# A four-layer decoder on one core: the order of instructions planned by a second simulator

## The chip, the core and the metric

The kernel runs as one program on one core of a Trainium2 chip. The time is the device time of one execution in microseconds. Before the change it was measured in 12 runs; one further execution was recorded with the hardware profiler, and all durations in this document come from such recorded executions.

## The reference

The input is `x`, 8 sequences of 256 tokens of 256 numbers, and a context `ctx_768` of 8 x 120 rows of 192 numbers. Four layers follow one another; each has a self-attention or its like, a cross-attention to the context, and a feed-forward part. After each of the twelve parts stands a residual sum and a layer norm:

```python
x = _layernorm(x + _L0_attn_ref(x, ...))
x = _layernorm(x + _L0_xattn_ref(x, ctx_768, ...))
x = _layernorm(x + _L0_ffn_ref(x, ...))      # 8 experts, the best one per token
...                                          # L1: rope attention, cross-attention, 32 experts and a shared one
...                                          # L2: attention with compressed keys, quantized cross-attention
x = _layernorm(x + _L2_ffn_ref(x, ...))
x = _layernorm(x + _L3_attn_ref(x, ...))
x = _layernorm(x + _L3_xattn_ref(x, ctx_768, ...))
x = _layernorm(x + _L3_ffn_ref(x, ...))      # fixed-point MLP with a piecewise linear gelu
```

The part that takes longest is layer 2's feed-forward. It looks up 4 heads x 8 experts of 4096 for each token by product keys, and adds a gated MLP:

```python
sx, ix = jax.lax.top_k(sim[0], TOPK)         # sim: queries against 128 keys, per half and head
sy, iy = jax.lax.top_k(sim[1], TOPK)
scores, pk = jax.lax.top_k(all_scores, TOPK) # all_scores: 8 x 8 sums of sx and sy
w = jnp.einsum('btd,bthkd->bthk', hidden_states, down_embed[indices])
w = jax.nn.silu(w) * jax.nn.softmax(scores, axis=-1)
experts_states = jnp.einsum('bthk,bthkd->btd', w, up_embed[indices])
mlp = jax.nn.silu(hidden_states @ Wg.T) * (hidden_states @ Wu.T) @ Wd.T
```

Layer 3's attention is a gated 3-tap convolution with a linear scan along the sequence and a layer norm of its own; its cross-attention has 8 heads of 64 on 120 context rows.

## The kernel before

**Tiles.** The 2048 tokens lie in 16 tiles of 128 tokens (`X`), with their transpose `xT` beside them. A batch is one sequence, two tiles. Matrix products go through `mm` (L144), transposes of X through `transpose_into_xT` (L185, copied by L186), and every part ends with `finish`: the sum of the residual, batch-norm statistics (L175, L176), a reciprocal root, X (L199) and its transposes. The reciprocal root is two POOL instructions (L153, L155) in the attention parts and a Newton iteration on DVE (L158 to L166) elsewhere.

**Who decides the order.** The program names operations in source order and writes no order of its own for the engines. A planner of the framework simulates the five engines and their queues: each engine takes, of the operations whose inputs are there by the simulated clocks, the one that stands first in the source. What comes out is a fixed list of instructions for PE, DVE, ACT, POOL and SP (the queue that issues most transfers), with waits on semaphores between them. On the chip each engine works off its own list in that order.

**The attention parts** (l0_attn, l1_attn, l1_xattn, l2_attn) run over pairs of heads' scores, sums and output products; before the scores' exponentials, each row's lower bound is transposed into the queries by `lower16` (L544), and after them sums are divided on DVE (`divided16`, L588 to L600) and projected (`project_o`, whose sum is L630).

**The border to l1_ffn.** In l1_xattn, `choose` (L764 to L768) takes the experts of each batch as soon as its X is there. At the same time ACT sums the absolute values of the quantized weights of l2_xattn (L800, L802). l1_ffn then adds these over partitions with one POOL instruction, `partition_all_reduce` (L1252); the steps that scale by it stand in `ternary` (L1983). `route1` (L1137 to L1235) makes the lists of tokens for 32 experts, and the experts follow: a gather of tokens (L988), two transposes (L1006), two products, and a store of y. Behind the loop, `prepare_l2_xattn` (L2015 to L2042) quantizes and multiplies the context for the next part, with transposes at L2040; `routed_batches` gathers the stored rows (L988, `w<-yd`) and adds them to X.

**l2_ffn** is one loop over the 8 batches with background work in generators:

```python
experts = self.expert_batches(w, spare[:, : 8 * D], pool, work, ps, general)
for b in range(B):
    experts(b, later)
    later = chain(convolve(b), attend(b))
```

In `batch(b, later)` stand the MLP's products, then for each of the two tiles groups of four gathered rows (L988): dot products with X (L1599), activation and weight (L1655, L1656), a diagonal matrix (L1660), and a product on PE that adds the row times its weight (L1661). Between these steps `next(later)` pulls the next piece of the background: first the routing of batch b + 1 (`route`: query products, `sim` by L1388, the best 8 by L1391 and L1392, and so on to L1468), then layer 3's convolution of batch b - 1 (`convolve`, called C below) and its cross-attention (`attend`, A below: score products L1781, their maximum L1789, exponentials L1792, transposes L1797, sums L1803). C0 and A0 are those of batch 0, and so on. The convolution and the attention share their buffers from batch to batch, one of each, so that C0, A0, C1, A1 ... C7, A7 are a serial chain. The fixed-point part (`fixed_point`, L1829) follows with units of half a batch.

The planner is given to the program in `kernel`, at the line that the diff changes:

## Time and profile before

| | us |
|---|---|
| median of 12 runs | 2550.86 |
| lowest and highest run | 2528.13, 2563.61 |
| profiled execution, whole | 2545.84 |
| its span | 2544.1 |
| PE busy | 2064.2 (81%) |
| DVE busy | 1549.6 (61%) |
| ACT busy | 933.6 (37%) |
| POOL busy | 681.4 (27%) |
| granted PE clock, mean | 0.88 |

A busy share is that of the time in which an instruction of the engine was running, over the span. A high share of the whole span can hide stages in which the engine waits, so the stages are looked at one by one. They were, by start and end in us: l0_attn 22 to 210, l0_xattn to 264, l0_ffn to 528, l1_attn to 750, l1_xattn to 922, l1_ffn to 1139, l2_attn to 1397, l2_xattn to 1547, the loop of l2_ffn to 2285, the rest of layer 3's attention parts to 2450 and the fixed-point part to 2545. The granted clock is the share of full speed that the TensorE was given in a stretch; matmul durations are longer where it is low.

### The profile page before, as it was taken

What the parts mean: (1) busy time and instruction counts of PE and PEld (TensorE: products, weight loads), DVE (VectorE), ACT (ScalarE), POOL (GpSimd) and SP (SyncE); (2) the same over time, 40 slices, a digit from 0 to 9 for tenths busy, and PEclk for the clock granted to TensorE, in tenths of its full rate; (3) what the DMA queues carried; (4) which work ended last, traced back from release to release, by engine and by line L of the source; (5) the groups of instructions that cost most, each with busy time, mean ns of one, the idle gap of its engine ahead of it and who ended that gap; (6) DMA issues with size and microseconds to landing.
All of it is one profiled execution on the core that took longest, in us unless ns stands there. A gap on an engine that the chain in (4) does not pass through costs nothing. (4 is left out here: it accounts for less than half of the span.)

```text
span 2544.1 us, 38544 instructions
## 1 busy us (share of the span) xinstructions
PE 2064.2 (81%) x14051; PEld 1505.8 (59%) x14051; DVE 1549.6 (61%) x5022; ACT 933.6 (37%) x2056; POOL 681.4 (27%) x731
## 2 busy tenths in 40 slices
PE   8998689699989978957787685778788888886885
PEld 5665588545557656824455433656666676665674
DVE  4666200276667756545666787774866875853775
ACT  2332233233334352212333242334443444442652
POOL 1022221221111205443321014333423423420232
PEclk9999699899999978968899786888888888896898
DMA  2001442200011116811100003112211211220000
GB/s 88 2 1 58 171 153 76 73 9 1 1 68 33 49 56 190 246 59 34 34 18 30 33 17 96 49 56 62 67 49 50 76 48 57 83 82 8 1 17 18
DMA packets 69045, 147.54 MB, mean 58 GB/s; under 512 B 15864, under 2 KB 39560, under 8 KB 66928
## 3 DMA queue, kind: packets, MB, share of 16 engines
q0 software_dynamic: 30528, 81.81, 10.9%
q1 hardware_dynamic: 35564, 59.47, 7.1%
q10 hardware_dynamic: 2756, 3.72, 0.4%
q8 instruction: 113, 1.85, 0.3%
q14 instruction: 84, 0.69, 0.1%
HBM read 175.56 MB, written 23.76 MB: 78 GB/s over the span
## 5 line engine op out<-in xcount | busy, mean ns | idle before, releaser
L988 POOL DMA_INDIRECT rows<-in_l2f_table_dram,index x240 | 248.1, 1034 | 301.5 <-PE po L1661 115.3
L144 PE MATMUL pp<-xT,w 128*128 128x256 f32 (+1 forms) x672 | 197.4, 439 | 4.6 <-DVE hT L1135 1.7
L144 PE MATMUL ph<-xeT,we 128*128 128x128 f32 (+1 forms) x992 | 175.8, 319 | 19.2 <-DMA we<-in_l0f_experts_dram,wrow 14.6
L185 PE MATMUL pt<-ident,X 128*128 128x128 f32 x352 | 78.7, 343 | 130.8 <-DVE X L199 113.0
L1661 PE MATMUL po<-rows,diag 128*128 128x256 f32 x480 | 142.7, 435 | 45.3 <-issue 29.8
L144 PEld LDWEIGHTS ph<-xeT,we 128*128 128x128 f32 x992 | 151.1, 200 | 40.7 <-DMA we<-in_l0f_experts_dram,wrow 15.9
L144 PEld LDWEIGHTS pp<-xT,w 128*128 128x128 f32 x672 | 140.6, 218 | 34.8 <-issue 7.2
L600 POOL TENSOR_TENSOR aT<-sides,inv 128x256 f32<-128x256 f32 x64 | 46.6, 729 | 421.3 <-DVE sides L598 327.8
L185 PEld LDWEIGHTS pt<-ident,X 128*128 128x128 f32 x352 | 49.7, 167 | 169.5 <-DVE X L199 80.8
L186 ACT COPY xT<-pt 128x512 f32<-128x512 f32 x88 | 51.4, 586 | 261.8 <-PE pt L185 257.5
L1661 PEld LDWEIGHTS po<-rows,diag 128*128 128x128 f32 x480 | 97.2, 214 | 76.3 <-issue 43.1
L988 POOL DMA_INDIRECT xe<-xd,take x87 | 86.2, 991 | 182.7 <-DVE y L1112 77.0
L144 PE MATMUL py<-we,hT 128*128 128x256 f32 x496 | 129.7, 386 | 1.2 <-DVE hT L1135 1.2
L1112 DVE TENSOR_TENSOR y<-py,we 128x256 f32<-128x256 f32 x23 | 9.8, 425 | 196.2 <-PE py L144 196.2
L564 ACT ACTIVATE e<-sc 128x512 f32<-128x512 f32 (+1 forms) x146 | 77.4, 602 | 99.7 <-PE sc L492 66.8
L1106 ACT ACTIVATE hT<-ph,we 128x128 f32<-128x128 f32 x184 | 65.7, 367 | 117.8 <-PE ph L144 86.1
L492 PE MATMUL sc<-kv,qv 32*128 32x128 f32 (+2 forms) x1520 | 103.6, 316 | 3.3 <-ACT e L564 1.9
L1660 ACT ACTIVATE diag<-ident,dots 128x128 f32<-128x128 f32 x224 | 75.4, 393 | 79.0 <-PE po L1661 22.2
L144 PE MATMUL sc<-xT,w 128*128 128x512 f32 x216 | 103.0, 626 | 1.3 <-ACT xT L186 1.3
L199 DVE TENSOR_SCALAR X<-z,ln_mv,rs_y 128x256 f32<-128x256 f32 x176 | 67.0, 423 | 58.5 <-POOL rs_y L155 58.1
L1599 DVE SCALAR_TENSOR_TENSOR junk<-rows,X 128x256 f32<-128x256 f32 x224 | 93.8, 419 | 12.7 <-DMA rows<-in_l2f_table_dram,index 7.0
L492 PEld LDWEIGHTS sc<-kv,qv 32*128 32x128 f32 x1520 | 80.2, 189 | 33.5 <-issue 26.2
(570 smaller groups left out, 5180.3 us busy)
## 6 DMA issues: line engine op xcount, KB each, us to landing
we<-in_l1f_experts_dram SPq DMA_DIRECT2D x32, 384.0 KB
yd<-y SPq DMA_DIRECT2D x32, 256.0 KB
w<-in_l2x_w_dram SPq DMA_DIRECT2D x1, 4096.0 KB
v<-v SPq DMA_DIRECT2D x16, 243.8 KB
rows<-in_l2f_table_dram,index POOLq DMA_INDIRECT x240
yd<-y SPq DMA_DIRECT2D x23, 128.0 KB
X<-in_x_dram SPq DMA_DIRECT2D x8, 256.0 KB
xd<-X ACTq DMA_DIRECT2D x8, 256.0 KB
```

Source lines behind the costliest of these rows:

```text
L144: self.nc.tensor.matmul(out, lhsT=lhsT, rhs=rhs, start=n == 0, stop=n == last and bias is None)
L185: nc.tensor.transpose(pt[:, c, j, :], self.X[:, i0 + j * step, c * P : (c + 1) * P], self.ident)
L186: nc.scalar.copy(self.xT4[:, :, i0 : i0 + step + 1 : step, :], pt)
L199: nc.vector.tensor_scalar(self.X[:, i, :], z[:, j, :], mv[:, j, 0:1], r[:, j : j + 1], ALU.subtract, ALU.mult)
L492: nc.tensor.matmul(sc[: shape[0], part], lhsT=lhsT, rhs=rhs, start=mask is None, stop=True, skip_group_check=True)
L564: lambda r, sc: nc.scalar.activation(e0[m][:n0, r], sc, AF.Exp),
L600: nc.gpsimd.tensor_tensor(out, split(both), split(inv), ALU.mult)
L988: self.nc.gpsimd.indirect_dma_start(out=out, out_offset=None, in_=table, in_offset=bass.IndirectOffsetOnAxis(ap=index, axis=0), **({} if r ...
L1106: nc.scalar.activation(hT[:, g + f, :], ph[:, f, :], AF.Gelu, bias=b1[:, g + f : g + f + 1])
L1599: nc.vector.scalar_tensor_tensor(junk, row, 1.0, x, ALU.mult, ALU.mult, accum_out=out)
L1660: nc.scalar.activation(diag, sel, AF.Copy, scale=dots[:, k : k + 1])
L1661: nc.tensor.matmul(po, lhsT=diag, rhs=rows[:, k, D:], start=False, stop=(g, k) == (groups[-1][0], size - 1))
```

## The change

The planner is told to use the framework's other simulator, the timeline simulator, when it decides which instruction comes next. No operation is added, removed or altered; the lists of instructions have the same operations in other orders, and with them other waits.

```diff
-    with tile.TileContext(nc) as tc:
+    with tile.TileContext(nc, schedule_with_timeline_sim=True) as tc:
         build(tc, ins, out)
```

How far instructions move in their engine's list, the two lists laid side by side: on PE, 1531 of the 1700 of the l2_ffn stage (by 59 places on average), 421 of 620 in l1_ffn (by 29), 216 of 257 in the fixed-point part (by 13), 253 of 439 in l2_xattn (by 4), and 227 to 417 of about 1100 in each attention part (by 1 to 2.5). On DVE, 1868 of 2094 in the l2_ffn stage (by 69). SP's list moves 13 of 212. POOL's moves little, but for the two tiles of a batch: before, the gathers of the second tile stand around POOL's steps of the next routing, after, behind them. The table loads of ACT go from 72 to 70.

## The prediction

> **What bounds the kernel now.** The page's busy table gives PE 81% of the span, DVE 61%, ACT 37%, POOL 27%. As the change moves order and nothing else, I needed to know stage by stage whether an engine is full (then order is worth little) or whether engines wait for each other (then order is worth what they wait). So the second view is the windows view, cut at the stage borders. The columns are the stretch in us, its length, busy us of PE, PEld, DVE, ACT and POOL, the granted PE clock, the DMA share and GB/s:
>
> ```profile
> 922.00:1139.00 217.00, 166.87 (x902) 128.56 (x903) 128.13 (x324) 60.17 (x138) 91.36 (x91) 0.82 0.53 157
> 1139.00:1397.00 258.00, 206.04 (x2064) 123.42 (x2062) 157.07 (x355) 88.91 (x152) 72.07 (x90) 0.89 0.09 26
> 1547.00:2285.00 738.00, 590.89 (x2728) 467.22 (x2726) 511.91 (x2410) 299.08 (x741) 272.02 (x261) 0.85 0.23 64
> 2285.00:2450.00 165.00, 127.61 (x555) 101.12 (x556) 97.94 (x241) 81.53 (x141) 22.86 (x12) 0.81 0.02 4
> ```
>
> These are l1_ffn, l2_attn, the l2_ffn loop, and what remains of layer 3's cross-attention behind it. The loop is 738 of 2544 us and no engine fills it: PE has 147 us free, DVE 226. Inside it the background chain C0, A0, C1, A1 ... C7, A7 (a convolution batch, then a context batch) is serial, and expert work is laid beside it. I cut the loop where each background batch starts on DVE. Two loaded phases (C4, A4) and two in which the chain runs almost alone (C6, A6):
>
> ```profile
> 2084.50:2135.60 51.10, 41.49 (x153) 31.40 (x152) 37.23 (x171) 18.63 (x54) 28.40 (x27) 0.80 0.29 82
> 2135.60:2180.80 45.20, 41.14 (x226) 32.53 (x225) 30.78 (x153) 21.15 (x47) 5.30 (x5) 0.92 0.13 38
> 2279.00:2302.00 23.00, 10.96 (x46) 7.87 (x44) 16.01 (x54) 4.51 (x11) 0.17 (x3) 0.86 0.00 0
> 2302.00:2345.00 43.00, 32.29 (x129) 24.37 (x129) 12.98 (x50) 11.59 (x29) 0.00 (x0) 0.62 0.05 12
> ```
>
> A context batch lasts 45 us loaded and 43 us alone: expert work beside it is nearly free. A convolution batch lasts 51 loaded and 23 alone. What is waited for in the loop is seen in the view of groups, by form (busy us, mean ns, idle us before and its releasers):
>
> ```profile
> L1661 PE MATMUL po<-rows,diag 128*128 128x256 f32 x480 | 142.7, 435 | 45.3 <-issue 29.8 <-ACT diag L1660 13.9 <-DMA rows<-in_l2f_table_dram,index 1.4
> L1391 DVE MAX8 top<-sim 128x8 f32<-128x128 f32 x128 | 32.0, 280 | 22.1 <-ACT sim L1388 21.8
> L1789 DVE TENSOR_REDUCE nm<-s 128x4 f32<-128x480 f32 x24 | 14.9, 650 | 18.7 <-PE s L1781 18.4
> ```
>
> **The l2_ffn loop.** In the changed order each batch's routing and its expert products stand one phase earlier against the chain; at the last expert product PE has passed C5 and A4 where before it had passed C6 and A5. On DVE the maximum of context scores (L1789) stands behind the batch's whole routing chain (L1391 to L1468). I counted the instructions of each phase in both orders and multiplied them by their mean durations in this trace. The larger of PE and DVE per phase, before/after, in us: up to C0 95/109.6; C0 65.5/46.1; A0 44.3/67.4; C1 51.4/44.2; A1 40.8/65.1; C2 44.5/46.5; A2 38.7/51.6; C3 44.5/41.9; A3 38.7/49.9; C4 44.5/36.7; A4 38.7/21.6; C5 45.5/26.3; A5 40.2/21.6. Before, these sum to 632.3 and the phases lasted 732.8: a factor of 1.16. After, the last three hold less than their latency. They cannot go below the rows of the chain alone: 43.5 for A4 and A5, 28 for C5 (23 alone plus its remaining expert work), 115 together. The ten loaded phases sum to 559.0.
> With 1.16 throughout that is 648 + 115 = 763, +30. By kind it is less: convolution phases lasted 1.07 times their larger sum before, context phases from A2 on 1.17, and the first phase was partly latency (127.5 for 95), so that I let half of its 14.6 more work show: 135 + 1.07 x 215.4 (C0 to C4) + 1.17 x 234.0 (A0 to A3) + 115 = 754, +21. I take **+20**. Ends: factor 1.05 (C0) gives 587 + 115 = 702, -31; 1.22 (A0 and A1 had 1.24 and 1.25) gives 797, +64. The loss has one cause: expert work is pulled forward out of A4, C5 and A5, where it was nearly free, into A0 and A1, which then have PE and DVE both at 65 and more.
> [...]
>
> **The end.** Behind the loop are C7, A7 and the fixed point's batches of some 20 us. After, the fixed point stands further ahead of A7 (parts of 5, 6 and 7 are left, before 3 to 7). The 165 us stretch has PE free for 37; a small part of that is got back: **-5** (-10 to 0).
>
> **The border to l1_ffn.** Before, POOL has batch 7's reciprocal root (L153, L155) ahead of the all-reduce (L1252), after behind it; and on DVE seven scalar steps (L1983) that wait for the all-reduce stand ahead of batch 7's last sum (L630), statistics and X. From the timeline view, DVE and then POOL (start, us, engine, line):
>
> ```profile
> 914.66 0.69 DVE L630 TENSOR_TENSOR z<-sc,biased 128x512 f32<-128x512 f32 x1 [3.82 <-PE sc L144]
> 917.48 0.73 DVE L199 TENSOR_SCALAR X<-z,ln_mv,rs_y 128x256 f32<-128x256 f32 x2 [1.13 <-POOL rs_y L155]
> ```
> ```profile
> 914.50 0.19 POOL L802 TENSOR_TENSOR w<-w,more 128x1 f32<-128x1 f32 x1 [2.86 <-ACT size L800]
> 916.44 0.22 POOL L153 TENSOR_SCALAR rs_v<-ln_mv 128x2 f32<-128x2 f32 x1 [1.75 <-DVE ln_mv L176]
> 923.15 0.49 POOL L1252 PARTITION_ALL_REDUCE w_scale<-w  x1 [5.71 <-issue]
> ```
>
> The all-reduce can start 5.71 us after L802 ends at 914.69 and is over at 920.9; seven steps of about 0.1 us bring L630 to 921.7 instead of 914.66: 7.0 later. Queued behind it are X, its transposes, the gate logits, L767 and the whole of route1; the experts' first gathers wait for that. After also loads POOL's other code once more between L1252 and L153; no row prices that, from 0 to another 5.71, which would put L153 at 926.6, 10.2 later. **+8**.
> [...]
>
> **The end of l1_ffn.** The changed order takes the preparation of the next cross-attention into the expert loop: 8 bit-linear products at 0.55 to 0.6 us, 16 transposes at L2040 of 0.43 and two small steps, 123.6 to 133.6 us of PE in a stretch (970 to 1086) where it is 111 of 116 busy. Before they lay from 1086 to 1107, under the last store and its gathers. Two groups of PE from 986 to 1130:
>
> ```profile
> L2040 PE MATMUL pp<-ident,w 128*120 128x128 f32 x16 | 3.9, 427 | 0.0
> L185 PE MATMUL pt<-ident,X 128*128 128x128 f32 x4 | 1.2, 448 | 14.4 <-DVE X L199 14.4
> ```
>
> That cover is given up and nothing takes its place: PE only waits longer at L185. **+9** (+4 if it first fills the 5 free us, +12 if DVE's conversions hold PE as well).
>
> **Attention stages.** 90 to 93% PE, and an instruction moves one to two places on average. The last transposes of lower16 (L544) go about 8 matmuls later. PE waits 12.0, 3.5 and 2.2 us there in l2_attn, l1_attn and l0_attn; half of 17.7 is **-8** (-15 to +5, as the late reciprocals could hold up the transposes). l0_ffn, l0_xattn and l2_xattn (DVE 124.6 of 150) keep their order but for a few places: 0 (-3 to +3). SP's queue moves 13 instructions; ACT's table loads go from 72 to 70 on the way, 3 us of ACT at most.
>
> **Sum.** 20 - 5 + 8 + 9 - 8 = +24 on the profiled 2545.84, 2570. The median of the runs is 5 above that execution, so against it the same step reads 2575.
>
> **Rivals.** *Faster:* the factor of the loop is no constant but the price of in-order waits that the other order avoids. For it: 29.8 of L1661's 45.3 us are "issue", PE waiting for nothing that shows, and L1391 and L1789 wait 40 us for engines which are not full. Against it: DVE's L1789 gets more work ahead of it, not less. Price: 1.05 gives -31 + 4 of the rest = -27, 2519. It decides from 1.084 down (-12 in the loop). *No change:* the chain sets both orders and the work moved forward is what idles anyhow; factor 1.085 to 1.11, 2546 (0.3% or 7.6 us is what a measurement can tell). *Slower by far:* routing ahead of L1789 stalls the chain each time, 1.22: +64 + 4 = 2614. That the change does nothing is excluded, as the queues differ: 1531 of 1700 PE instructions of the loop are moved.
>
> **Chances.** Forecast (2554 to 2595) 0.46, far slower 0.14, no change 0.11, faster 0.29. Range 2510 to 2630: the ends of the loop with the smaller terms on the same side in part. The sign hangs on the loop's factor: 1.084 is the point, the phases of before show 1.05 to 1.25 and 1.16 as their mean, so most of the chance lies above. The forecast's own range has the loop at +4 to +45.
>
> **What would show it.** Right: A4, C5 and A5 at PE under 0.7 busy with 43, 28 and 43 us and the last expert product before A5; A0 and A1 at 70 to 80 us; L630 of batch 7 some 7 us later against the stage's start; PE idle at L185 after l1_ffn above 14.4. Wrong: A0 and A1 under 68, L1661's idle below 20, the loop (first routing to C6) at 705 or less. If the attention stages move by over 15 us, the terms of places were mis-sized.

## The result, and the profile after

The changed kernel takes 2699.58 us (median of 11 runs, 2693.51 to 2705.60), the kernel before 2547.9 (46 runs): a ratio of 1.0597 [1.0578, 1.0616], 6% slower. The forecast was 2570, its range 2510 to 2630: the direction was right, the size was missed by 130 us. The profiled execution took 2701.38 us.

```profile
PE 2222.5 (82%) x14051; PEld 1622.7 (60%) x14051; DVE 1561.5 (58%) x5022; ACT 935.8 (35%) x2054; POOL 682.8 (25%) x731
```

The first thing to see is this line of the page. No operation was added, and DVE, ACT and POOL are busy within 12 us of before, but PE is busy 158 us more (2222.5 for 2064.2). PE does not wait more (477.0 us of its span idle, before 479.9); it is at work for longer with the same 14051 instructions.

Where? The windows view of the changed kernel, cut at l1_attn, l1_ffn with l2_attn, and the loop of l2_ffn (the columns are those of the prediction), and below it l1_attn of before, whose line was not shown:

```profile
542.00:813.00 271.00, 262.56 (x2048) 159.72 (x2046) 142.61 (x296) 87.15 (x158) 41.53 (x56) 0.88 0.02 9
1172.00:1516.00 344.00, 283.82 (x2123) 162.78 (x2121) 171.84 (x401) 92.46 (x158) 96.04 (x116) 0.82 0.11 31
1656.00:2434.00 778.00, 615.85 (x2723) 500.08 (x2722) 520.97 (x2408) 300.11 (x739) 272.28 (x261) 0.81 0.21 61
```
```profile
528.00:750.00 222.00, 205.85 (x2039) 125.80 (x2037) 142.94 (x295) 85.13 (x153) 41.49 (x52) 0.99 0.02 6
```

In l1_attn PE has the same 2040 instructions, 57 us more of busy time, and 0.88 of the clock where it had 0.99. All stages of the two recorded executions, in us, cut at the last ACT instruction of each (so that l1_ffn ends at 1107 before, and what follows up to 1139 counts with l2_attn):

| stage | before | after | difference | forecast |
|---|---|---|---|---|
| start | 22 | 16 | -6 | 0 |
| l0_attn | 190 | 202 | +12 | in -8 |
| l0_xattn | 51 | 43 | -8 | 0 |
| l0_ffn | 266 | 282 | +16 | 0 |
| l1_attn | 223 | 272 | +49 | in -8 |
| l1_xattn, with part of the border | 170 | 181 | +11 | in -8, +8 |
| l1_ffn and l2_attn | 476 | 520 | +44 | +9, in -8 |
| l2_xattn | 150 | 144 | -6 | 0 |
| l2_ffn and the end | 996 | 1040 | +44 | +20 - 5 |

**Attention: the rotation of the row groups.** `four_banks` writes two kinds of products. Masks (L487) are 128*128 in the profile's lines, all rows of the PE array; score products (L492) are 32*128, one of four row groups, and the source issues four masks and then score products that take the four row groups in turn. The profile has two instructions for each score product (1024 in l1_attn for the program's 512). From the timeline view (start, us, engine, line, tile and the number of instructions that follow one another), before and then after:

```profile
537.49 0.61 PE L487 MATMUL sc<-causal,ident_bf 128*128 128x256 bf16 x4
538.03 1.15 PE L492 MATMUL sc<-kv,qv 32*128 32x256 f32 x16
```
```profile
554.92 0.28 PE L487 MATMUL sc<-causal,ident_bf 128*128 128x256 bf16 x1
555.13 1.13 PE L492 MATMUL sc<-kv,qv 32*128 32x256 f32 x4
...
577.23 0.39 PE L487 MATMUL sc<-later_k,ident_bf 128*128 128x256 bf16 x1
577.55 2.07 PE L492 MATMUL sc<-qv,kv 32*128 32x256 f32 x4
```

Before, 16 instructions of 32x256, which the program gives to the four row groups in turn, take 1.15 us. After, the timeline planner puts a mask, the four instructions of one row group, the next mask, and so on: these 4 alone take 1.13 us, so that the 16 before ran side by side. And 22 us later four of one row group take 2.07. The windows view of after shows the clock around that place, 0.91 up to 562 us and 0.50 behind it:

```profile
553.00:562.00 9.00, 8.03 (x53) 5.39 (x53) 6.97 (x12) 0.10 (x1) 0.00 (x0) 0.91 0.00 0
562.00:592.00 30.00, 30.00 (x136) 18.13 (x134) 6.96 (x11) 4.48 (x9) 0.00 (x0) 0.50 0.00 1
592.00:772.00 180.00, 178.05 (x1650) 107.52 (x1648) 114.06 (x234) 66.04 (x120) 29.44 (x36) 0.99 0.01 1
```

From 562 to 592 PE is busy in all of the 30 us, and its clock is 0.50. In l1_attn and l1_xattn together, counted in steps of 3 us, PE runs 87 us below 0.75 while it is over 90% busy; before it was 18. Without such windows the loss is seen where busy time is compared at equal counts, in the groups of PE in l1_attn, before and then after:

```profile
L492 PE MATMUL sc<-qv,kv 32*128 32x128 f32 (+1 forms) x408 | 27.9, 342 | 0.1
```
```profile
L492 PE MATMUL sc<-qv,kv 32*128 32x128 f32 (+1 forms) x408 | 50.6, 396 | 0.0
```

The mean of one instruction rises only from 342 to 396 ns, as instructions that overlap are each counted whole (408 of 342 ns are 139.5 us, in 27.9 us of busy time); the group's busy time rises from 27.9 to 50.6 us. In the two programs' lists I counted rounds, a round being successive 32-row products none of which uses a row group a second time, and switches between products of the whole array and those of a part. l1_attn has 512 such products, so 128 rounds at least: before 131 rounds and 128 switches, after 197 and 208. Over the four attention parts after has 199 more rounds and 202 more switches.

**The loop.** Two groups of the loop that the prediction showed, after (L1661 had waited 45.3 us, 29.8 of them for "issue", and L1789 18.7):

```profile
L1661 PE MATMUL po<-rows,diag 128*128 128x256 f32 x480 | 132.5, 411 | 21.5 <-issue 11.1 <-ACT diag L1660 10.3
L1789 DVE TENSOR_REDUCE nm<-s 128x4 f32<-128x480 f32 x24 | 15.2, 648 | 13.4 <-PE s L1781 13.1
```

Both wait less, and still the loop from the first routing to C6 lasts 777.2 us, before 732.8. By phase, from C0: 41.5, 81.6, 46.3, 75.2, 43.5, 63.0, 43.0, 62.0, 45.4, A4 50.4, C5 37.5, A5 42.7. PE is also busy for longer at equal counts, 616 us for 591, at a clock of 0.81 for 0.85; whether these 25 us or the waits come first was not separated. The chain is served late. A3 of after begins at 2194.1; from its timeline, PE, ACT and DVE:

```profile
2202.09 3.62 PE L144 MATMUL s<-xT,w 128*128 128x256 f32 x16
2207.99 0.70 PE L1781 MATMUL s<-kT,qT 64*128 64x120 f32 x4 [2.29 <-ACT qT L1774]
...
2204.72 1.28 ACT L1134 ACT_TABLE_LOAD   x1
2207.35 1.08 ACT L1774 ACTIVATE qT<-s 128x512 f32<-128x512 f32 x2
...
2213.51 0.64 DVE L1789 TENSOR_REDUCE nm<-s 128x4 f32<-128x480 f32 x1
```

Its first products stand behind ten instructions of MLP products on PE, its query copy (L1774) behind two table loads and a silu on ACT, and its maximum behind the routing chain on DVE, which works through L1435 to L1496 from 2204.7 to 2213.6. The first maximum starts 19.4 us after the start of the phase, in before's A3 9.45.

**The border.** POOL and then DVE of after:

```profile
982.73 0.49 POOL L1252 PARTITION_ALL_REDUCE w_scale<-w  x1 [5.65 <-issue]
990.09 0.24 POOL L153 TENSOR_SCALAR rs_v<-ln_mv 128x2 f32<-128x2 f32 x1 [6.88 <-issue]
```
```profile
983.69 0.68 DVE L630 TENSOR_TENSOR z<-sc,biased 128x512 f32<-128x512 f32 x1
991.20 0.74 DVE L199 TENSOR_SCALAR X<-z,ln_mv,rs_y 128x256 f32<-128x256 f32 x2 [5.83 <-POOL rs_y L155]
```

L630 stands 8.2 us behind L802's start where it stood 0.2 behind it; then POOL waits 6.88 us for nothing that shows ahead of L153. route1 begins 20.8 us after the end of L802, before 8.1.

### The profile page after: what moved, and what is told of

Its sections match the earlier page's. It is cut to its first block, busy times and chain, and to the rows that moved or that the text cites. A ratio compares the mean times of both kernels' runs of the same rounds, so it can differ in the third digit from the quotient of the medians.

```text
span 2699.5 us, 38557 instructions
## 1 busy us (share of the span) xinstructions
PE 2222.5 (82%) x14051; PEld 1622.7 (60%) x14051; DVE 1561.5 (58%) x5022; ACT 935.8 (35%) x2054; POOL 682.8 (25%) x731
## 5 line engine op out<-in xcount | busy, mean ns | idle before, releaser
L144 PE MATMUL pp<-xT,w 128*128 128x256 f32 (+1 forms) x672 | 184.7, 423 | 8.3 <-DVE hT L1135 6.9
L185 PE MATMUL pt<-ident,X 128*128 128x128 f32 x352 | 76.8, 346 | 116.7 <-DVE X L199 109.1
L600 POOL TENSOR_TENSOR aT<-sides,inv 128x256 f32<-128x256 f32 x64 | 46.6, 729 | 463.8 <-DVE sides L598 411.9
L1661 PE MATMUL po<-rows,diag 128*128 128x256 f32 x480 | 132.5, 411 | 21.5 <-issue 11.1
L492 PE MATMUL sc<-kv,qv 32*128 32x128 f32 (+2 forms) x1520 | 144.2, 338 | 0.7 <-DVE sides L598 0.7
L185 PEld LDWEIGHTS pt<-ident,X 128*128 128x128 f32 x352 | 50.3, 170 | 148.3 <-issue 82.8
L492 PE MATMUL sc<-qv,kv 32*128 32x128 f32 (+2 forms) x1352 | 138.1, 366 | 0.0
L492 PEld LDWEIGHTS sc<-kv,qv 32*128 32x128 f32 x1520 | 108.4, 205 | 31.2 <-issue 24.4
L1661 PEld LDWEIGHTS po<-rows,diag 128*128 128x128 f32 x480 | 95.1, 205 | 42.6 <-issue 14.8
L492 PEld LDWEIGHTS sc<-qv,kv 32*128 32x128 f32 (+1 forms) x1352 | 91.8, 202 | 30.4 <-issue 22.1
```

Of the source, the lines that this page charges most:

```text
L144: self.nc.tensor.matmul(out, lhsT=lhsT, rhs=rhs, start=n == 0, stop=n == last and bias is None)
L185: nc.tensor.transpose(pt[:, c, j, :], self.X[:, i0 + j * step, c * P : (c + 1) * P], self.ident)
L492: nc.tensor.matmul(sc[: shape[0], part], lhsT=lhsT, rhs=rhs, start=mask is None, stop=True, skip_group_check=True)
L600: nc.gpsimd.tensor_tensor(out, split(both), split(inv), ALU.mult)
L1661: nc.tensor.matmul(po, lhsT=diag, rhs=rows[:, k, D:], start=False, stop=(g, k) == (groups[-1][0], size - 1))
```

## The experiments

The five sets ran on four chips, and the time of before itself is not the same in all of them: 2554.63, 2453.41, 2451.57, 2544.48 and 2544.54 us. In a kernel that was recorded in two sets (`mix` below) most of the difference lies in the l2_ffn loop. Each kernel is therefore compared with before of its own set, and stage times only within a set or with the set named. The theories in the expectations go by letters: A is the lost rotation, D the prediction's own cause (expert work pulled forward into the wrong phases), G that the clock falls to half where one row group is alone at work, J that no single queue carries the loop's loss, K that rotation, border and loop are all of it; other letters are their rivals.

### Is it the rotation?

`pin_banks` is the changed kernel, with the products of one call of `four_banks` held in source order by dependencies of order alone:

```diff
+        run = self.in_order()          # each product after the one before, on the same queue
         if mask is not None:
             for sc in banks:
-                nc.tensor.matmul(
+                run(nc.tensor.matmul(
...
         for parts in zip(*(heads(r) for r in range(4))):
             for sc, (part, lhsT, rhs) in zip(banks, parts):
-                nc.tensor.matmul(
+                run(nc.tensor.matmul(
```

> The changed kernel (timeline planner), with the matmuls of each four_banks call chained on PE in source order (masks, then the row groups 0, 32, 64, 96 in turn), issue order only. Theory A (the new order broke the rotation over the four 32-row groups of the PE array, so that matmuls which ran side by side run one after another): l1_attn back from 271 to about 225 us, l2_attn from 297 to about 260, l0_attn and l1_xattn some 10 shorter each, granted clock in l1_attn back from 0.88 to above 0.95, in all about 110 less: 2590. Rival B (the loss of the attention parts is in what waits on DVE and ACT, not in PE's order): within 15 us of the changed kernel, 2700.

Measured: 2615.02 us, 1.0227 [1.0195, 1.0259] of before; 2590 was expected. Rounds and switches are back at 129 and 136 in l1_attn, the stage at 227 us with a clock of 0.98, l0_attn at 193. The comparison with after was made later within one set:

> The changed kernel unaltered, beside its variants on one chip: 1.06 of the kernel before on a chip where that takes 2550; where it takes 2450, the kernels that keep this loop order have lost 105 us in the loop instead of 44, so 1.08 to 1.09 (2640 to 2680).

> pin_banks beside the changed kernel on one chip: 80 to 95 us below it, all of it in l0_attn, l1_attn, l1_xattn and l2_attn.

Measured: 2697.07 (1.0582 [1.0517, 1.0647]) and 2608.38 (1.0255 [1.0222, 1.0287]). The rotation is worth 89 of the 153 us that after loses there: l0_attn 207 to 193, l1_attn 266 to 229, l2_attn 346 to 313, while the loop stays (775.5 and 779.1).

### What the rotation's loss is made of

Four kernels with the order of the planner before, in which only `four_banks` differs. `bank_by_bank` issues all score products of one row group before those of the next; `half_masks` splits each mask in two and issues both halves first, as the control for `masks_between`, which puts the second halves in the middle of the products; `mask_and_bank` issues a mask, then all products of its row group, and so on, which is the pattern seen at 555 us. In `half_masks` the first half of each mask does not enter the sums.

```diff
 # bank_by_bank
-        for parts in zip(*(heads(r) for r in range(4))):
-            for sc, (part, lhsT, rhs) in zip(banks, parts):
+        for sc, parts in zip(banks, (heads(r) for r in range(4))):
+            for part, lhsT, rhs in parts:
 # half_masks                             # masks_between
+        masks(0)                          +  for at, parts in enumerate(...):
+        masks(1)                          +      if at % n == 0: masks(at // n)
 # mask_and_bank: bank_by_bank, with each mask directly ahead of its row group's products
```

> The kernel before (default planner), four_banks written bank by bank: all matmuls of row group 0, then of 32, 64, 96, chained on PE; the switches between full-array and 32-row matmuls stay as they were. Theory A: each attention part 40 to 100 us longer (the changed kernel lost 50 in l1_attn with a quarter of the broken rounds), in all +150 to +350: 2700 to 2900, with the granted clock of these parts down to 0.9 or less. Rival C (the switches between full-array and 32-row matmuls cost the time, not the rotation): within 15 us of before, 2550.

> Control for the next: the kernel before, each mask matmul of four_banks cut into two halves, all of them ahead of the 32-row matmuls, chained on PE; no more switches than before. All theories: 8 short mask matmuls instead of 4 longer ones per call, +10 to +30 us in all.

> As half_masks, but the second half of the masks stands in the middle of the 32-row matmuls: some 240 more switches between full-array and 32-row matmuls in the four attention parts, the rotation over the row groups untouched. Theory A: within 25 us of half_masks (0.1 us for a switch). Rival C (a switch costs what the changed kernel lost per added switch, 114 us over 202 more switches, 0.56 us): 130 us above half_masks.

> The kernel before (default planner), four_banks written as mask, then the matmuls of its bank, bank by bank, chained on PE: both faults at once, as the changed kernel has them in some places. If the prices of bank_by_bank (0.13 us per broken round, 1200 more here) and masks_between (0.17 us per switch, 650 more here) simply add: about +270, 2820, clock in l1_attn 0.95 as there. Theory G (a stretch in which only a quarter of the array works makes the chip grant half the clock although PE is busy throughout): l1_attn's clock below 0.7 and well above 2820, up to 3200.

Measured: `bank_by_bank` 2672.78, 1.0449 [1.0414, 1.0484]: 118 us for 915 more rounds, 0.13 us each, less than expected. Its clock in l1_attn is 0.96; for 18 of 252 us there, in steps of 3 us, PE is over 90% busy with the clock below 0.75, before for 3, so that the price of a round holds some of that lower clock already. `half_masks` 2554.96, 1.0008 [0.9987, 1.0030]; `masks_between` 2594.84, 1.0157 [1.0123, 1.0190]: 40 us over its control for 256 more switches, 0.16 us each, between what the two theories had (25 at most, at a guess of 0.1 us a switch that no run had shown, and 130). At these prices after's 199 rounds and 202 switches make 26 + 32 = 58 of the 89 us.

`mask_and_bank` took 3341.06, 1.3642 [1.3606, 1.3678]: 888 us more, three times what the two prices give for its 1299 more rounds and 741 more switches (168 + 116 = 284). Its windows, l1_attn as a whole and twelve us of it:

```profile
763.00:1321.00 558.00, 555.38 (x2043) 345.45 (x2042) 151.02 (x293) 94.06 (x157) 41.22 (x55) 0.63 0.01 3
```
```profile
900.00:912.00 12.00, 12.00 (x27) 6.42 (x26) 2.12 (x4) 1.19 (x2) 0.00 (x0) 0.50 0.00 0
```

l1_attn lasts 558 us for 223, PE is busy in 555 of them, and in 417 of them the clock is below 0.75. So with the two faults together the clock is below 0.75 for three quarters of the stage, where `bank_by_bank` has 18 us of it and `masks_between`, at 234 us, a mean clock of 0.99. The 31 us that the prices leave of after's 89 fit its stretches below 0.75: 87 us in l1_attn and l1_xattn and, with PE at 90% or more, 69 in l2_attn, where before has 18 and 27. Of the 111 us more, 55 would be lost if all of them ran at the 0.50 of the window above, an upper estimate. That the stretches cost those 31 is worked out so, not measured by itself, and a part may stand in the 26 for the rounds already.

What the runs show of PE's array is this: 16 products of the four row groups in the time of 4 of one (1.15 and 1.13 us), 0.16 us for a switch between products of the whole array and those of a part (`masks_between`), and a clock of 0.50 through 30.00 us in which the profile has PE busy for all 30.00. What lowers the clock was not measured.

### The loop: phases, or the queues' order?

`pin_throttle` was to hold the expert work of the changed order back to the phases of before: the query products of batch b's routing are issued after the first products of A(b-3), those of its MLP after the last of C(b-2). `pin_border` instead tries the border (the all-reduce marked to keep its program order) and holds `prepare_l2_xattn` behind the last expert product; `pin_all` does all of it. All three have the rotation pinned.

```diff
 # pin_throttle
+   with self.behind(("A", o // CH - 3)):   self.mm(pp[:, n, :], ...)   # routing's queries
+   with self.behind(("C", b - 2)):         self.mm(pp[:, n, :], ...)   # MLP
 # pin_border
+   tc.keep_in_program_order(nc.gpsimd.partition_all_reduce(self.w_scale, ...))
+   with tc.issue_after(last.ins):          self.prepare_l2_xattn(pool, ps2)
```

> pin_banks, and in the l2_ffn loop the routing of batch k is issued on PE only behind the first product of A(k-3), the MLP of batch b behind the output product of C(b-2), which are about the places they had before. Theory D (the loop lost its time because expert work is pulled one phase forward and A4, C5, A5 run nearly empty): the loop falls by 35 to 50 us, A0 and A1 to 55 us, in all about 2573. Rival E (the order inside the phases does it, whatever phase the work stands in): within 10 us of pin_banks, 2615.

> pin_banks, with the all-reduce (L1252) kept behind all earlier POOL instructions and the preparation of the next cross-attention issued on PE behind the last expert's product, as before. Theory F (batch 7's root behind the all-reduce and its two code loads costs 12.7 us, the preparation inside the expert loop about 9): 20 to 24 us below pin_banks, about 2593. Rival: other work hides both, within 6 us of pin_banks.

> All three together: pinned banks, the throttled loop, the border and the late preparation, under the timeline planner. If the three causes are separate and complete: 2550 to 2560, no difference from before that is left to explain but some 6 us in l0_ffn. If it stays above 2575 a cause is missing.

Measured: 2589.34 (1.0561 [1.0541, 1.0582]), 2594.84 (1.0576 [1.0556, 1.0597]) and 2610.33 (1.0646 [1.0628, 1.0664]). Compared by their ratios, as before took 2453 in this set and not the 2550 that the expectations had, all three miss. The loop of `pin_throttle` lasts 772 us, and 761 in `pin_border`, which is not throttled. But the throttle did not bring back the phases of before. Its C3 and A3, which lasted 45.6 and 45.3 us before:

```profile
2019.10:2049.60 30.50, 19.55 (x87) 15.56 (x85) 23.55 (x92) 11.22 (x35) 20.56 (x20) 0.95 0.38 101
2049.60:2126.20 76.60, 66.07 (x295) 53.44 (x295) 48.22 (x232) 31.69 (x67) 13.27 (x13) 0.77 0.11 33
```

Of a batch's 80 PE instructions for routing queries and first MLP products (`pp<-xT,w`), A1 to A4 of `pin_throttle` hold 64 each, where before they held 23 to 34 and the C phases the rest; A0 and A1 last 79 and 76 us, not 55. So the run gathers the work in the A phases even more, and says nothing for or against the prediction's cause. `pin_border` did not move the all-reduce (route1 still starts 21.7 us after L802), and its late preparation made l1_ffn and l2_attn together 497 us, for 477 in `pin_throttle`: in this order the preparation was cheaper in the expert loop than behind it.

The next kernels put back whole lists, and with them the phases and the order inside them. They have the rotation pinned and give some engines of l2_ffn the order of before, as a list of instructions chained one after the other:

```diff
+        pin_orders(tc)        # ORDERS: the lists of before for l2_ffn
 # loop_dve: DVE     loop_pe: PE     loop_pe_dve: PE and DVE     loop_all: PE, DVE, ACT and POOL
```

> pin_banks, with DVE's order in the l2_ffn stage chained to that of the kernel before (issue order only); PE, ACT and POOL stay free for the timeline planner. pin_throttle showed that moving the work by a phase is not the cause. Theory H (each step of the serial chain C, A stands in a queue behind routing and expert steps that are in no hurry, above all on DVE): the loop, first routing to C6, falls to within 15 us of the kernel before, 35 us or more below border_root of this series. Rival I (PE's queue is what serves the chain late): it stays within 10 us of border_root's.

> As loop_dve, with the orders of PE, DVE, ACT and POOL in the l2_ffn stage chained to those of before. Both theories: the loop and the end as in the kernel before; what is left against before is the border and l1_ffn and the first gathers of l0_ffn, 20 to 35 us in all.

> pin_banks, with PE's order alone in the l2_ffn stage chained to that of before. Theory I (the chain C, A is served late in PE's queue: in A3 of the changed kernel its first products stand behind the products of an MLP): the loop comes within 20 us of before's, far below the 734 us of loop_dve. Theory J (no single queue: the chain crosses PE, ACT and DVE some 40 times per batch and is late wherever one of the queues is in the other order): the loop stays over 700 us on a chip where before has 650, as loop_dve did.

> As loop_pe, with DVE's order too; ACT and POOL free. Theory J: most of the way to loop_all (654 us), 670 to 690. Theory I: the same as loop_pe.

Measured: `loop_dve` 2562.98 (1.0463 [1.0444, 1.0482]) and `loop_all` 2477.56 (1.0105 [1.0087, 1.0123]) in one set; `loop_pe` 2663.21 (1.0475 [1.0432, 1.0518]) and `loop_pe_dve` 2589.29 (1.0194 [1.0153, 1.0234]) in the set of `pin_banks_again`. The windows of the loop, first `border_root` (below; the changed order) and `loop_all`, then `pin_banks_again` (the changed order) and `loop_pe`:

```profile
1539.00:2294.00 755.00, 609.95 (x2719) 497.72 (x2717) 517.90 (x2406) 298.58 (x737) 274.27 (x262) 0.81 0.22 64
```
```profile
1554.00:2208.00 654.00, 550.96 (x2709) 446.64 (x2707) 505.79 (x2404) 294.87 (x736) 273.26 (x257) 0.90 0.26 72
```
```profile
1560.00:2339.00 779.00, 612.54 (x2721) 496.44 (x2719) 518.64 (x2407) 298.87 (x737) 273.75 (x262) 0.82 0.22 62
```
```profile
1563.00:2390.00 827.00, 603.08 (x2703) 474.43 (x2702) 512.49 (x2402) 323.19 (x751) 267.92 (x257) 0.82 0.20 57
```

All four lists put back bring 101 us in that set, of a loop of 755; PE is busy 59 us less at equal counts, at a clock of 0.90 for 0.81. DVE's alone bring 22 (733.8); PE's alone cost 47 (826.5 for 779.1): PE now waits 61.8 us for X (L199) of DVE and 39.9 for its `over` (L1459 of before), where it waited 25.3 and 25.0. PE's and DVE's bring 20 (759.6).

`loop_pe_dve` is the test of the phases that `pin_throttle` was not: from C0 to A5 the work on PE and DVE stands phase by phase as before, to within a few instructions, and still 25 us are missing to the 734.6 that all four lists reach in a set with the same time of before (`put_back`, below). So the phases of PE's and DVE's work by themselves bring back no more than 20 us, and the rest comes only with the lists of ACT and POOL; neither of those was put back alone. PE's list or DVE's by itself does not carry the loss, and theories H and I fall; J's 670 to 690 for `loop_pe_dve` missed too. One queue of one plan among three of another can be worse than either plan.

### The border, and the account as a whole

`border_root` issues the all-reduce after the last reciprocal root of l1_xattn; rotation pinned, nothing else.

```diff
-            y, v = ...; nc.gpsimd.tensor_tensor(y, v, self.half[:, :n], ALU.pow)
+            self.last_root = nc.gpsimd.tensor_tensor(y, v, self.half[:, :n], ALU.pow)
...
+            with tc.issue_after(self.last_root.ins):
                 nc.gpsimd.partition_all_reduce(self.w_scale, self.w_sums[:, : len(L2X)], P, bass_isa.ReduceOp.add)
```

> pin_banks, with the all-reduce (L1252) issued on POOL behind batch 7's root (L155), as before; pin_border had left it ahead (route1 began 21.5 us after L802 there too). Theory: route1 begins 8 us after L802 instead of 21, and the time falls by 10 to 13 us against pin_banks on a chip of the same kind. If other work hides it: l1_ffn's last expert comes as late as in pin_banks, 197 to 203 us after L802.

Measured: 2563.38, 1.0459 [1.0441, 1.0476]. route1 starts 14.4 us after L802 (21 in `loop_dve` and `loop_all`), not the 8 expected; l1_xattn lasts 167 us for their 176, before 170. The set has no `pin_banks`, so that the whole gain was not measured. `put_back` joins everything: rotation, the all-reduce after the root, and l1_ffn and l2_ffn in the lists of before, the rest as the timeline planner has it. `mix` goes the other way: the planner of before, with start, l0_attn, l0_xattn and l2_xattn in the lists of `pin_banks`.

> The changed planner, but four_banks keeps its rotation, the all-reduce is issued after the last reciprocal root, and the l1_ffn and l2_ffn stages have the engines' orders of before. Theory K (rotation, the border with l1_ffn, and the loop's orders are the whole loss): what is left of the changed order is l0_ffn's later first gathers (+7 to +14), and its gains at the start, in l0_xattn and in l2_xattn (6, 5 to 8 and 7 together 18 to 20), some of the pinned attention stages' small differences (0 to +5): ratio 0.994 to 1.005 against before on the same chip. Theory L (a part of the loss is still unnamed, as the same orders cost more behind other ones): 1.01 and more. On its way: the loop from the first routing to C6 within 10 us of that of before, route1 14 us or less after L802.

> Default planner, banks pinned, and two stretches chained to the orders that pin_banks has under the timeline planner: from the start to the end of l0_xattn (263 us before, 254 there) and l2_xattn (150 before, 142 there). If stages are independent: 12 to 17 us below the kernel before, a ratio of 0.993 to 0.996.

> The planner of before, with the attention parts' banks in rotation and the stages from the start to l0_xattn, and l2_xattn, in the orders of the changed planner with the rotation kept. Before on another chip it took 0.9923 of before, 19 us less. If that came from these stages alone it is the same here: 15 to 22 us less, ratio 0.991 to 0.994, with the start 6, l0_xattn 5 to 8 and l2_xattn 7 us shorter and the other stages within 3. If the gain came with that chip's shorter loop, it is under 10 here.

Measured: `put_back` 2542.91, 0.9988 [0.9968, 1.0007], as theory K had it. Its l1_attn (226 us) and its loop are close to those of the recorded execution of before:

```profile
1541.00:2276.00 735.00, 585.71 (x2708) 464.07 (x2707) 509.20 (x2403) 296.52 (x736) 271.28 (x257) 0.86 0.23 64
```

The account is not closed to the last, though: `mix_again`, in the same set, has the same gains at the start, in l0_xattn and l2_xattn and the planner of before elsewhere, and takes 19 us less than `put_back` by the medians. In the recorded executions 5 us of it are l0_ffn's later first gathers (277 us for 272), and the loop lasts 735 us for 718; why, stays open. `mix` took 2431.93, 0.9923 [0.9908, 0.9939] and, on another chip, 2524.16, 0.9934 [0.9915, 0.9952]: 20 us less than before both times by the medians, by the ratio the fastest version of this study. Its start is 6 us shorter, l0_xattn 5, l2_xattn 7 to 9.

## Why the prediction was right or wrong

**Attention stages, -8 predicted: this step failed.** The working was "an instruction moves one to two places on average", with half of PE's waits at L544 as the gain. The measured effect is +89 (`changed_again` against `pin_banks_again`). The distance that an instruction moves was the wrong measure: one mask that moves two places stands between two row groups, and then the products of one row group run alone instead of side by side. Nor were all four stages "90 to 93% PE": the prediction's own row of l2_attn has 206 of 258 us, 80%. The trace of before had what was needed, `32*128` in the form of the products and 16 instructions of them in 1.15 us; only how many row groups each stretch of the new list keeps busy was not counted. The last of the prediction's marks named this: over 15 us in the attention stages means mis-sized terms of places.

**The loop, +20 predicted, +44 measured: the work moved as forecast, but its price was not the whole.** A0 and A1 hold 72 and 64 us of PE's work, before 49 and 44, and last 81.6 and 75.2, at and above the forecast 70 to 80. The factor held: without the last three phases the loop took 777.2 - 130.6 = 646.6 us for a larger-engine sum of 559.0, 1.157 for the 1.16 of the plain reckoning. The reckoning by kind of phase, which was taken, had 639 for them, 7 less, and A4, C5 and A5 lasted 50.4, 37.5 and 42.7, 15.6 more than the 115 put down for them; 21 + 7 + 16 is the 44. The step that failed is "the loss has one cause": only PE and DVE were counted, and with the work of both back in the phases of before `loop_pe_dve` regains only 20 us. The lists of ACT and POOL, put at nothing, hold some 25 (`put_back` against `loop_pe_dve`, two sets with the same time of before). In A3 the chain's steps were seen to stand late on PE, ACT and DVE; which waits make the sum stays open. That the factor fitted says little for the cause.

**The border, +8 predicted, +12.7 measured at route1.** L630 came 8.0 later against L802, forecast 7.0. After's list has the second load of POOL's code between L1252 and L153, its trace two MODIFY_POOL_CONFIG of L153 there, at 983.2, and then the 6.88 us in which POOL waits for nothing that shows, 5.65 ahead of L1252; +8 lay between no second wait (7.0) and a full one (10.2). The 2.5 us above 10.2 are 1.4 of a POOL step (L600) and its wait, which now stand between L802 and the all-reduce, and 1.2 of a second wait longer than 5.71.

**The end of l1_ffn, +9 predicted, +9.6 measured by the same cut.** From route1's first step to the last expert product 162.4 us became 175.8, and from there to the first product of l2_attn 47.1 became 43.3. That fits the term, a longer expert loop and a tail that hardly shrinks; `put_back`, with l1_ffn's lists of before, has 163.4 and 47.1. The wait was foretold at the wrong place: PE waits 8.0 us for the stored rows (`w<-yd`, L1331), before not at all, while L185's longest wait rose from 14.4 to 16.2 but over equal counts stayed (16.6 before). That the preparation alone makes the difference is not shown: `pin_border`, which holds back its products on PE only, has 171 and 54.

**The end, -5 predicted; others, 0 predicted.** From C6 to the last X, 252.6 us for 251.0: nothing came back. The start, l0_xattn and l2_xattn gained 6, 8 and 6 us and l0_ffn lost 16, so that "a few places" was wrong for each of them and nearly right for their sum, -4.

## What to carry to other kernels

A reordering is not measured by how far instructions move, but by what it does to things that only work in company: here products of different row groups, 16 of which take 1.15 us side by side and 4 of one group alone 1.13, and lists of several engines that were planned together. Where an order carries speed, as the rotation does here (89 us), it should be pinned in the kernel and not be left to a planner. And PE was busy here in all of 30 us while its clock was 0.50; compare a group's busy time at equal counts, and read the granted clock beside the busy share.

## What was not expected of the hardware

The half clock under full load is one: 0.50 for 30 us with PE busy throughout, and 0.63 on average over a stage of 558 us in `mask_and_bank`, where before has 223. What lowers it was not measured.

The other is that the l2_ffn loop has two lengths for one and the same program: `mix` took 651.0 us for it in one set and 718.3 in another. The product that adds the gathered rows shows it, in the groups of the first and then of the second (its line is shifted by the edit, L1661 of before):

```profile
L1678 PE MATMUL po<-rows,diag 128*128 128x256 f32 x480 | 125.9, 401 | 11.8 <-ACT diag L1677 11.7
```
```profile
L1678 PE MATMUL po<-rows,diag 128*128 128x256 f32 x480 | 138.4, 422 | 43.1 <-issue 18.4 <-ACT diag L1677 17.2 <-DMA rows<-in_l2f_table_dram,index 7.0
```

Where the loop is short, the waits of "issue" and for the gathered rows are gone, and the clock from l2_ffn's start to the end is 0.89 for 0.86. The stretch from l1_ffn's last expert product to l2_attn, which gathers rows too, has two lengths as well, 35.9 and 47.1 us. One chip gave both times of before, 2453.41 and 2544.54, in different sets, so that it is not the chip alone; the cause stays open. It matters for the loop's price, 44 us in the recorded executions and 101 in the set where the loop is short: with the order of before the loop is some 80 us shorter there (`loop_all` 654 for `put_back` 735), with the changed order only some 20 (755.5 for 775.5 to 779.1).
